# Adjacency turned by the DMA engines from a bf16 DRAM scratch, in place of TensorE turns through PSUM

## Chip, cores, metric

One NeuronCore of a Trainium2 chip runs the whole program. Times are device microseconds of that core; lower is better. Each kernel has four to nine runs, and its median is quoted. Ratios are the mean time of one kernel's fast runs over that of the other's of the same rounds, so not quite the ratio of the medians.

## The reference, cut to what matters

A stack of four graph attention layers over 16 graphs of 1024 nodes with 256 features. All layers of a graph use the same 1024 x 1024 adjacency, given as int32.

```python
# layers 0 to 2, each (activation and slope differ):
e = act(f1[:, :, None] + f2[:, None, :])          # (B, N, N)
e = where(adj == 0, -inf, e);  att = softmax(e, -1)
x = x + einsum('bij,bjo->bio', att, h)
# layer 3: the same with four heads, then a layer norm for each head
```

The kernel keeps attention weights with the neighbour j on the partitions, so it needs the mask turned: `mask[j, i]` from `adj[i, j]`. The adjacency of this input is symmetric, but the kernel may not count on it.

## The kernel before

The turn lies in `load`. A tile of 128 rows is loaded and cast to bf16 by the DMA, ScalarE sums (a - 0.5)^2 as a check that all entries are 0 or 1, TensorE turns eight 128 x 128 blocks into PSUM, and ScalarE copies them to the uint8 mask.

```python
def load(b):
    xs[b] = nodes.tile([P, NI, D], F32, name="x_b")
    nc.sync.dma_start(xs[b], x[b]...)
    masks[b] = nodes.tile([P, NI, N], U8, name="mask")      # three buffers
    def fetch(i):
        fetched[i] = adjs.tile([P, N], BF, name="adj_i")    # three buffers
        nc.gpsimd.dma_start(fetched[i], adj[b, ts(i, P), :])
    for i in range(AHEAD): fetch(i)                         # AHEAD = 2
    yield
    for i in range(NI):                                     # NI = 8
        if i + AHEAD < NI: fetch(i + AHEAD)
        adj_i = fetched.pop(i)
        every = wide.tile([P, N], BF, name="wide")
        nc.scalar.activation(every, adj_i, AF.Square, bias=minus_half,
                             accum_out=squares[:, b, i : i + 1])
        turned = psum.tile([P, NI, P], BF, name="misc", bufs=3)
        for j in range(NI):
            nc.tensor.transpose(turned[:, j, :], adj_i[:, ts(j, P)], ident_b)
        nc.scalar.copy(masks[b][:, :, ts(i, P)], turned)
        yield
```

`load(b + 2)` is advanced one step at each of the eight head steps of layer 3 of batch b. Two batches run interleaved. Instructions of an engine run in the order in which the program was built, and that order is not the program text's: work is placed where it was expected to be ready.

```python
# weigh: on VectorE, 8 of these for a half of 512 nodes
nc.vector.scalar_tensor_tensor(w[:, j, :], r, c(j), mask[:, j, ts(half, HALF)],
                               op0=op, op1=ALU.mult)                    # L255
# project: GpSimd makes 1/sqrt(var), ScalarE copies the turned activations (hT)
nc.gpsimd.tensor_tensor(r, r, minus_half.to_broadcast([P, n]), op=ALU.pow)   # L212
nc.scalar.copy(hT, turned)                                                   # L232
# layer 3, head step n
accT = ...8 matmuls...;  nc.scalar.copy(sums, accT);  next(coming, None);  yield 7.5
acc = ...4 turns of sums...;  inv = small.tile([P, NG], F32, name="inv4")
inverse(inv, acc[:, :, E])
```

Of the kernel before, what the change touches and what calls it, by code (L numbers as in the profile page):

```python
# [32 lines left out]
BF = mybir.dt.bfloat16  # L33
# [3 lines left out]
AF = mybir.ActivationFunctionType  # L37
# [3 lines left out]
P = 128  # L41
# [17 lines left out]
def short_path(ctx: ExitStack, tc: tile.TileContext, ins: dict, out: bass.AP, bad: bass.AP):  # L59

    nc = tc.nc
    x, adj = ins["x"], ins["adj"]
    B, N, D = x.shape
    H, T, E = ins["L3_a_src"].shape
    NI = N // P
# [5 lines left out]
    AHEAD = 2  # L71
    LAG = 120.0

    const = ctx.enter_context(tc.tile_pool(name="const", bufs=1))
    nodes = ctx.enter_context(tc.tile_pool(name="nodes", bufs=3))
    adjs = ctx.enter_context(tc.tile_pool(name="adjs", bufs=3))
    wide = ctx.enter_context(tc.tile_pool(name="wide", bufs=3))
    psum = ctx.enter_context(tc.tile_pool(name="psum", bufs=2, space=bass.MemoryType.PSUM))

    ident = const.tile([P, P], F32, name="ident")  # L80
    make_identity(nc, ident)
    ident_b = const.tile([P, P], BF, name="ident_b")
    nc.vector.tensor_copy(ident_b, ident)
    minus_half = const.tile([P, 1], F32, name="minus_half")
    nc.vector.memset(minus_half, -0.5)
    ones = const.tile([P, P], F32, name="ones")
# [2 lines left out]
    squares = const.tile([P, B, NI], F32, name="squares")  # L89
# [3 lines left out]
    xs, masks = {}, {}  # L93

    def load(b: int):

        xs[b] = nodes.tile([P, NI, D], F32, name="x_b")
        nc.sync.dma_start(xs[b], x[b].rearrange("(i p) f -> p i f", p=P))
        masks[b] = nodes.tile([P, NI, N], U8, name="mask")
        fetched = {}  # L100

        def fetch(i: int):

            fetched[i] = adjs.tile([P, N], BF, name="adj_i")
            nc.gpsimd.dma_start(fetched[i], adj[b, ts(i, P), :])  # L105

        for i in range(AHEAD):
            fetch(i)
        yield
        for i in range(NI):  # L110
            if i + AHEAD < NI:
                fetch(i + AHEAD)
            adj_i = fetched.pop(i)

            every = wide.tile([P, N], BF, name="wide")
            nc.scalar.activation(
                every, adj_i, AF.Square, bias=minus_half, accum_out=squares[:, b, i : i + 1]
            )
            turned = psum.tile([P, NI, P], BF, name="misc", bufs=3)
            for j in range(NI):  # L120
                nc.tensor.transpose(turned[:, j, :], adj_i[:, ts(j, P)], ident_b)
            nc.scalar.copy(masks[b][:, :, ts(i, P)], turned)
            yield


# [8 lines left out]
    bias = const.tile([P, D], F32, name="bias")  # L134
# [4 lines left out]
    for _ in load(0):  # L139
        pass  # L140
# [136 lines left out]
    def batch(b: int):  # L277
        xb, mask = xs.pop(b), masks.pop(b)
        coming = load(b + 2) if b + 2 < B else iter(())

        def begin(l: int):
# [164 lines left out]
    def stream(first: int):  # L446
        if first:
            for _ in load(first):
                yield 2.0
        for b in range(first, B, 2):  # L450
            yield from batch(b)
# [314 lines left out]
def tile_gat4(  # L766
# [27 lines left out]
    nc.vector.memset(ones, 1.0)  # L794
    n_bad = flags.tile([1, 1], I32, name="n_bad")
    short_path(tc, ins, out, bad)
    with tc.tile_pool(name="flag_psum", bufs=1, space=bass.MemoryType.PSUM) as psum:
        bads = psum.tile([1, 1], F32, name="bads")
# [39 lines left out]
```

## Time and profile before

| | before |
|---|---|
| median | 3343.4 us (3341.4 to 3344.3) |
| profiled span | 3341.3 us |
| first attention weights (L255) begin | 44.5 us |
| first output store issued | 360.3 us |
| from there to the end | 2981.0 us |

The prediction below shows the lines of the profile that it rests on.

### The profile page before, as it was taken

What the parts mean: (1) busy time and instruction counts of PE and PEld (TensorE: products, weight loads), DVE (VectorE), ACT (ScalarE), POOL (GpSimd) and SP (SyncE); (2) the same over time, 40 slices, a digit from 0 to 9 for tenths busy, and PEclk for the clock granted to TensorE, in tenths of its full rate; (3) what the DMA queues carried; (4) which work ended last, traced back from release to release, by engine and by line L of the source; (5) the groups of instructions that cost most, each with busy time, mean ns of one, the idle gap of its engine ahead of it and who ended that gap; (6) DMA issues with size and microseconds to landing.
All of it is one profiled execution on the core that took longest, in us unless ns stands there. A gap on an engine that the chain in (4) does not pass through costs nothing.

```text
span 3341.3 us, 38569 instructions
## 1 busy us (share of the span) xinstructions
PE 3103.0 (93%) x13702; PEld 2107.8 (63%) x13702; DVE 2504.0 (75%) x6140; ACT 974.3 (29%) x2081; POOL 1091.2 (33%) x1286
## 2 busy tenths in 40 slices
PE   6899999999989999899998999989999899998987
PEld 5765756657656675665756667566666666656652
DVE  5677787777778777787777877778777787777766
ACT  3423323232232322323233232332323223232121
POOL 1223324233242332424234142242323423234242
PEclk9999999999999999999999999999999999999998
DMA  4101101011010110101011010010101101000000
GB/s 115 26 4 16 32 11 40 7 17 29 13 39 8 16 29 13 38 10 16 26 16 35 10 42 4 13 35 13 39 4 17 32 13 38 7 10 13 1 13 14
DMA packets 55192, 73.19 MB, mean 22 GB/s; under 512 B 4049, under 2 KB 37969, under 8 KB 54993
## 3 DMA queue, kind: packets, MB, share of 16 engines
q0 software_dynamic: 18432, 33.56, 6.7%
q1 hardware_dynamic: 36560, 37.10, 3.5%
q8 instruction: 110, 1.80, 0.2%
q14 instruction: 90, 0.73, 0.1%
HBM read 87.43 MB, written 16.78 MB: 31 GB/s over the span
## 4 chain that ended last, share of the span: by engine, by line
DVE 45%; PE 42%; POOL 5%; ACT 4%; issue 3%; DMA 1%; SPq 0%; ACTq 0%; POOLq 0%; DVEq 0%
DVE weights L255 25%; PE acc L338 18%; PE acc L414 11%; PE projected L236 10%; DVE above L226 3%; PE misc L230 3%; DVE above L273 2%; DVE stats L220 2%; DVE above L274 2%; POOL x_b L275 2%; DVE V L290 2%; DVE y L380 1%; POOL y L379 1%; POOL rstd L212 1%; ACT below L271 1%
## 5 line engine op out<-in xcount | busy, mean ns | idle before, releaser
L338 PE MATMUL acc<-V,weights 128*128 128x257 f32 x6144 | 1454.9, 385 | 12.5 <-DVE weights L255 11.5
L338 PEld LDWEIGHTS acc<-V,weights 128*128 128x128 f32 x6144 | 1137.8, 191 | 208.9 <-DVE weights L255 47.2
L414 PE MATMUL acc<-weights,V 128*65 128x512 f32 x2048 | 914.2, 593 | 0.3 <-DVE weights L255 0.3
L255 DVE SCALAR_TENSOR_TENSOR weights<-row,ex,mask 128x512 f32<-128x512 f32 x1024 | 762.7, 784 | 2.7 <-ACT row L251 0.9
L255 DVE SCALAR_TENSOR_TENSOR weights<-row,V,mask 128x512 f32<-128x512 f32 x768 | 559.4, 776 | 53.0 <-ACT row L251 52.9
L414 PEld LDWEIGHTS acc<-weights,V 128*65 128x65 f32 x2048 | 278.7, 138 | 492.7 <-issue 474.0
L212 POOL TENSOR_TENSOR rstd<-rstd,minus_half 128x2 f32<-128x2 f32 (+1 forms) x320 | 311.3, 975 | 745.7 <-DVE rstd L211 703.2
L236 PE MATMUL projected<-W,hT 128*128 128x259 f32 (+1 forms) x2048 | 521.8, 398 | 14.8 <-ACT hT L232 11.3
L236 PEld LDWEIGHTS projected<-W,hT 128*128 128x128 f32 x2048 | 383.5, 195 | 130.1 <-ACT hT L232 60.4
L275 POOL TENSOR_TENSOR x_b<-x_b,above 128x256 f32<-128x256 f32 x256 | 227.5, 890 | 585.8 <-DVE above L274 532.5
L230 PE MATMUL misc<-ident,above 128*128 128x128 f32 x1024 | 189.1, 289 | 155.3 <-DVE above L226 108.6
L271 ACT ACTIVATE below<-acc,inv 128x256 f32<-128x256 f32 x256 | 120.0, 472 | 607.4 <-DVE inv L264 497.0
L232 ACT COPY hT<-misc 128x512 f32<-128x512 f32 x256 | 149.1, 586 | 495.8 <-PE misc L230 494.8
L230 PEld LDWEIGHTS misc<-ident,above 128*128 128x128 f32 x1024 | 113.7, 143 | 256.0 <-DVE above L226 120.3
L220 DVE BATCH_NORM_STATS2 stats<-x_b 128x6 f32<-128x256 f32 x512 | 206.7, 414 | 83.1 <-POOL x_b L275 78.9
L263 DVE TENSOR_SCALAR inv<-acc 128x1 f32<-128x1 f32 x256 | 37.3, 150 | 272.5 <-PE acc L338 272.3
L418 ACT COPY sums<-acc 65x512 f32<-65x512 f32 x128 | 74.0, 578 | 546.2 <-PE acc L414 546.1
L226 DVE TENSOR_SCALAR above<-x_b,mv 128x256 f32<-128x256 f32 x512 | 222.0, 443 | 3.8 <-POOL x_b L275 1.7
L105 POOL DMA_DIRECT2D adj_i<-in_adj_dram x128 | 77.1, 603 | 406.3 <-ACT sums L418 174.4
L290 DVE TENSOR_SCALAR V<-projected,rstd,V 128x256 f32<-128x256 f32 x256 | 134.8, 537 | 63.9 <-ACT V L286 62.9
L286 ACT ACTIVATE V<-projected,rstd 128x3 f32<-128x3 f32 x384 | 99.4, 261 | 262.0 <-PE projected L236 220.1
L314 POOL TENSOR_TENSOR x_b<-x_b,beta 128x256 f32<-128x256 f32 x128 | 117.3, 923 | 150.7 <-DVE above L226 148.6
(70 smaller groups left out, 2370.1 us busy)
## 6 DMA issues: line engine op xcount, KB each, us to landing
adj_i<-in_adj_dram POOLq DMA_DIRECT2D x128, 256.0 KB, 3.8
x_b<-in_x_dram SPq DMA_DIRECT2D x16, 1024.0 KB, 7.8
out_dram<-y SPq DMA_DIRECT2D x32, 512.0 KB, 3.8
W<-in_L_gnn_W_dram SPq DMA_DIRECT2D x3, 256.0 KB, 3.0
a_b<-in_L_gnn_a_dram SPq DMA_DIRECT2D x3, 256.0 KB, 6.4
a_b<-in_L_gnn_a_src_dram SPq DMA_DIRECT2D x1, 640.0 KB, 7.5
a_b<-in_L_gnn_a_dst_dram SPq DMA_DIRECT2D x1, 640.0 KB, 9.4
W<-in_L_gnn_W_dram SPq DMA_DIRECT2D x2, 128.0 KB, 8.9
```

What stands on the lines that cost most here:

```text
L212: nc.gpsimd.tensor_tensor(r, r, minus_half.to_broadcast([P, n]), op=ALU.pow)
L220: nc.vector.bn_stats(stats, xb[:, 2 * pair + n, :])
L226: nc.vector.tensor_scalar(above, xb[:, 2 * pair + n, :], mv[:, n, 0:1], 0.0, op0=ALU.subtract, op1=ALU.max)
L230: nc.tensor.transpose(turned[:, k, ts(n, P)], above[:, ts(k, P)], ident)
L232: nc.scalar.copy(hT, turned)
L236: nc.tensor.matmul(projected, hT[:, k, ts(n, P)], W[l][:, k, :], start=(k == 0), stop=(k == NK - 1),)
L255: nc.vector.scalar_tensor_tensor(w[:, j, :], r, c(j), mask[:, j, ts(half, HALF)], op0=op, op1=ALU.mult)
L271: nc.scalar.activation(below, acc[:, :D], AF.Exp, scale=inv)
L275: nc.gpsimd.tensor_add(xi, xi, above)
L290: nc.vector.tensor_scalar(V[:, i, :D], projected[:, :D], rstd, V[:, i, D : D + 1], op0=ALU.mult, op1=ALU.mult,)
L338: nc.tensor.matmul(acc, w[:, j, ts(i % NG, P)], V[:, j, : D + 1], start=(j == 0), stop=(j == NI - 1),)
L414: nc.tensor.matmul(accT, V3[:, j, h, :], w[:, j, :], start=(j == 0), stop=(j == NI - 1))
```

## The change

The intent is to free TensorE, the fullest engine, of 1024 turns, and ScalarE of reading PSUM, and to let the idle DMA engines turn. A cast to bf16 goes from DRAM to a DRAM scratch (four casts for a batch, issued by GpSimd). SyncE then issues eight turned loads of it. One such load of 128 columns by 1024 rows is called a strip here. A strip reads all rows, so it needs all four casts.

```diff
--- before.py
+++ after.py
@@ -76,11 +76,10 @@
     adjs = ctx.enter_context(tc.tile_pool(name="adjs", bufs=3))
     wide = ctx.enter_context(tc.tile_pool(name="wide", bufs=3))
     psum = ctx.enter_context(tc.tile_pool(name="psum", bufs=2, space=bass.MemoryType.PSUM))
+    dram = ctx.enter_context(tc.tile_pool(name="dram", bufs=2, space=bass.MemoryType.DRAM))
 
     ident = const.tile([P, P], F32, name="ident")
     make_identity(nc, ident)
-    ident_b = const.tile([P, P], BF, name="ident_b")
-    nc.vector.tensor_copy(ident_b, ident)
     minus_half = const.tile([P, 1], F32, name="minus_half")
     nc.vector.memset(minus_half, -0.5)
     ones = const.tile([P, P], F32, name="ones")
@@ -97,29 +96,29 @@
         xs[b] = nodes.tile([P, NI, D], F32, name="x_b")
         nc.sync.dma_start(xs[b], x[b].rearrange("(i p) f -> p i f", p=P))
         masks[b] = nodes.tile([P, NI, N], U8, name="mask")
+
+        narrow = dram.tile([N, N], BF, name="narrow")
+        for q in range(4):
+            nc.gpsimd.dma_start(narrow[ts(q, 2 * P), :], adj[b, ts(q, 2 * P), :])
         fetched = {}
 
-        def fetch(i: int):
-
-            fetched[i] = adjs.tile([P, N], BF, name="adj_i")
-            nc.gpsimd.dma_start(fetched[i], adj[b, ts(i, P), :])
-
-        for i in range(AHEAD):
-            fetch(i)
+        def fetch(j: int):
+            fetched[j] = adjs.tile([P, N], BF, name="adj_j")
+            nc.sync.dma_start_transpose(fetched[j], narrow[:, ts(j, P)])
+
         yield
-        for i in range(NI):
-            if i + AHEAD < NI:
-                fetch(i + AHEAD)
-            adj_i = fetched.pop(i)
+        for j in range(AHEAD):
+            fetch(j)
+        for j in range(NI):
+            if j + AHEAD < NI:
+                fetch(j + AHEAD)
+            adj_j = fetched.pop(j)
 
             every = wide.tile([P, N], BF, name="wide")
             nc.scalar.activation(
-                every, adj_i, AF.Square, bias=minus_half, accum_out=squares[:, b, i : i + 1]
-            )
-            turned = psum.tile([P, NI, P], BF, name="misc", bufs=3)
-            for j in range(NI):
-                nc.tensor.transpose(turned[:, j, :], adj_i[:, ts(j, P)], ident_b)
-            nc.scalar.copy(masks[b][:, :, ts(i, P)], turned)
+                every, adj_j, AF.Square, bias=minus_half, accum_out=squares[:, b, j : j + 1]
+            )
+            nc.scalar.copy(masks[b][:, j, :], adj_j)
             yield
 
 
```

## The prediction

> **What bounds the kernel now.** I read the page's engine totals first, then the totals by window, the groups by line, the waits of TensorE, and the timeline around one group of turns.
>
> ```profile
> PE 3103.0 (93%) x13702; PEld 2107.8 (63%) x13702; DVE 2504.0 (75%) x6140; ACT 974.3 (29%) x2081; POOL 1091.2 (33%) x1286
> ...
> DVE 45%; PE 42%; POOL 5%; ACT 4%; issue 3%; DMA 1%; SPq 0%; ACTq 0%; POOLq 0%; DVEq 0%
> ```
>
> TensorE is busy 93% of the span, yet the chain that ended last passes as often over VectorE (45%) as over TensorE (42%). So TensorE is the fullest engine, but time taken off it is not all time taken off the end: part turns into waits for VectorE. ScalarE (29%) and GpSimd (33%) have room.
>
> ```profile
> 0.00:45.00 45.00, 18.59 (x113) 15.58 (x114) 18.11 (x87) 25.31 (x41) 9.93 (x21) 1.00 0.82 213
> 45.00:3341.00 3296.00, 3084.44 (x13591) 2092.18 (x13589) 2485.86 (x6054) 949.00 (x2040) 1081.30 (x1265) 0.99 0.09 19
> ```
>
> The windows (columns: TensorE, its weight loads, VectorE, ScalarE, GpSimd, clock, DMA share, GB/s) show two regimes. In the first 45 us the DMA engines are 82% busy and TensorE has little to do: the start is a load. After that TensorE is 3084.44/3296 = 93.6% busy, with some 212 us idle, and the DMA engines are 9% busy. There is a great deal of DMA room for a turn that moves there.
>
> ```profile
> L121 PE MATMUL misc<-ident_b,adj_i 128*128 128x128 bf16 x1024 | 86.2, 226 | 27.2 <-DVE ident_b L83 13.8 <-DMA adj_i<-in_adj_dram 12.9 <-ACT row L251 0.5
> L116 ACT ACTIVATE wide<-adj_i,minus_half 128x1024 bf16<-128x1024 bf16 x128 | 145.7, 1138 | 7.4 <-DMA adj_i<-in_adj_dram 7.4
> L122 ACT CAST mask<-misc 128x1024 uint8<-128x1024 bf16 x128 | 128.8, 1008 | 63.4 <-PE misc L121 63.4
> ```
>
> The turns that go away are L121: 1024 of them, 226 ns in the record. That duration is not what one costs, because matmuls overlap. The timeline of TensorE around one group shows the real price:
>
> ```profile
> 639.69 1.88 PE L414 MATMUL acc<-weights,V 128*65 128x512 f32 x4
> 641.41 0.61 PE L121 MATMUL misc<-ident_b,adj_i 128*128 128x128 bf16 x8
> 641.86 1.95 PE L338 MATMUL acc<-V,weights 128*128 128x257 f32 x8
> ```
>
> The eight turns start at 641.41 and the next matmul starts at 641.86: 0.45 us for eight, 56 ns for one. Other whole groups repeat this 0.447 us.
>
> ```profile
> PE misc L230 <- DVE above L226: 108.6, 129, 3.1
> PE misc L230 <- DVE mv L221: 29.0, 13, 2.8
> ...
> PE misc L230 <- ACT mask L122: 1.9, 1, 1.9
> PE misc L423 <- ACT mask L122: 1.8, 7, 0.3
> ```
>
> TensorE's waits after 50 us (total us, times, longest) are nearly all for the layer norm on VectorE ahead of the turns of L230. Waiting for the PSUM buffer that the mask copy of L122 holds is a few us in all.
>
> **What the Trainium skill says.** (1) "VectorE: DVE Perf Modes", section "The three transpose paths": a 128x128 bf16 turn is given 390 ns on TensorE and 1309 ns by the DMA crossbar. The trace has 226 ns for one on TensorE and a pitch of only 56 ns inside a stream, so the table's 390 ns overstates what this change removes about sevenfold. (2) "DMA: Bandwidth & Descriptors", section "Latency and other measured facts", gives the DMA transpose 261 GB/s where the middle dimension isn't contiguous. The two disagree: by (2) a 1024x128 turn (262 KB) is 1.0 us of data, by (1) taken eight times it is 10.5 us. No transpose is in the trace of before, so nothing decides. (3) Same page, section "Anatomy of one DMA — SWDGE (gpsimd) path": about 2.0 us fixed plus bytes over 436 GB/s. For one tile of adjacency (512 KB read) that is 3.2 us; the trace says 3.8 us to landing, near enough. (4) Same page, section "Two DMAs through the same engine are not ordered": the transpose may be issued only after the cast's completion is seen, so their latencies add. Every turned column strip reads all 1024 rows, so it waits for all four casts of its batch.
>
> **The change part by part.**
>
> Removed from TensorE: 1024 turns x 56 ns = 57 us in all, of which 960 lie after the start (the profile counts 960 after 40 us): 960 x 56 ns = 54 us. Not all comes off the end: with 212 us idle already there and VectorE on 45% of the chain, I choose 60 to 65% as realised, between 48% (TensorE's part of TensorE plus VectorE on the chain, 42 of 87) and the 93.6% that its occupancy suggests. That is -34 us.
>
> Removed waits: no adjacency turn occupies a "misc" PSUM buffer any more. The waits for L122 seen on TensorE and its loads are 1.9 + 1.8 + 1.8 and 3.5 + 3.5 + 2.2 us, the pairs overlapping, so about 6 us. -5 us.
>
> ScalarE: the mask copy reads SBUF bf16 in place of PSUM. L116 does the same size from SBUF in 1138 ns against 1008 ns for L122, so at most 128 x 0.13 = +17 us on an engine idle 71% of the time. 0 us on the path. The squares are summed over columns in place of rows, at the same cost.
>
> GpSimd: 128 issues of 603 ns become 64 of twice the rows. At the worst twice the time each, so 77 us stays 77 us, off the path. Its waits ahead of L105 (406.3 us in the page) fall away, but where I looked the next GpSimd instruction was released by VectorE after that, so they cost nothing. 0 us.
>
> DMA: the casts took 6.7% of sixteen engines' span, 224 us, 14 us a batch. They now write DRAM. To these come 128 turned strips, 1.0 us each by (2), 10.5 us by (1); I take 2.5 us as an estimate between the two, weighted to the first: 8 x 2.5 = 20 us a batch. Together about 34 us of DMA time in a batch's 3341/16 = 209 us. Even at 10.5 us it would be 98 us, and fit. The throughput is hidden.
>
> Latency in the steady state: ScalarE runs in order, and the squares and mask copies of a batch wait for casts (14 us or more) and then the strips. In the trace of before, the first squares of a batch ran at 563.73 and their mask copy at 642.09, so such work is placed tens of us ahead of need. If the order built for the new kernel places a square slightly before its strip lands, ScalarE stands still, and behind it are row copies and hT copies that TensorE and VectorE need. I put 2 us of stall on each of 16 batches, of which a third counts: 16 x 0.7 = +11 us.
>
> Start: before, the adjacency tiles came one after another, the last mask copy of batch 0 began at 34.17 us, and the first weights (L255) at 44.52, eight of them spread to about 50. Now the four casts share busy DMA engines with W, x and the constants: landing at 22 to 25 us. Then eight strips at 2.5 us, +3 us of first latency and 2 us for ScalarE: 24 + 20 + 3 + 2 = 49 us for the last mask. It is needed at about 50, so nearly all of the 15 us fits in slack, while the x and a loads that share the engines come later. I put +8 us.
>
> Sum: 3343.65 - 34 - 5 + 0 + 11 + 8 = 3323.65. Call it **3323 us**, 0.6% faster.
>
> **Rivals.** A: the gain is realised in full and nothing is given back (ScalarE's slack hides everything). For it: TensorE 93.6% busy after the start, DMA 9%. Against it: the VectorE half of the chain. It makes 3343.65 - 57 - 6 = 3281 us, still within 2%. To be over 2% faster it would need more than TensorE spends on these turns, by a better order of everything else.
>
> B: the DMA turn is as slow as the table's 1309 ns a block. Then eight strips are 84 us, the start is longer by 24 + 84 + 5 - 50 = about 63 us, and each batch stalls ScalarE by much more: at 10 us counted a batch +160 us. With -39 us gained that is around 3343 + 63 + 160 - 39 = 3527 us, slower by 5%. For it: the skill's table. Against it: the bandwidth figure of the other page, and that the work lies far ahead of its use.
>
> C: VectorE's chain alone sets the end, and TensorE's 54 us all turn into waiting on L226 and L255. Then only the start counts: 3343 + 8 + 11 - 5 = 3357 us. For it: VectorE first on the chain with weights L255 alone 25%. Against it: TensorE idle only 6.4% after the start, and its waits for L255 only 11.5 us.
>
> **Range and chances.** Rival A bounds the fast side at 3281; a lucky order may give 15 us more: low 3266. The slow side holds C and a mild form of B, where the start costs 30 us and stalls 50 us: 3343 + 80 - 39 = 3384, rounded up: high 3395. Faster by over 2% (under 3276.8) 0.09; slower by over 2% (over 3410.5), which is B, 0.14; within 2% 0.77.
>
> **What would show each step.** TensorE's busy time after should fall to about 3103 - 86 = 3017 us, with L121 gone and the span falling by less. The waits of L230 for L226 should grow by some 20 us over 108.6; if they grow by 50, C was right. ScalarE's waits for the DMA of adj_j after the start should be under 40 us; hundreds would be B. The landing of one strip should be 3 to 6 us from issue; over 10 is B. The first weights (L255) should begin by 55 us. The prediction is wrong if the strips land much later than that, if SyncE holds strips behind output stores, or if the new order of instructions moves other waits by more than 60 us.

## The result, and the profile after

The changed kernel takes 3472.3 us (3462.1 to 3477.5, four runs), a ratio of 1.0383 (95% interval 1.0357 to 1.0408): 3.8% slower, outside the range that the prediction gave. The page of the changed kernel, its busy times, its chain, its DMA queues and its DMA issues:

```profile
PE 3051.4 (88%) x12678; PEld 2059.0 (59%) x12678; DVE 2496.7 (72%) x6139; ACT 980.9 (28%) x2081; POOL 1042.0 (30%) x1222
...
q1 hardware_dynamic: 171728, 70.67, 8.8%
q0 software_dynamic: 2048, 33.56, 4.5%
...
DVE 40%; PE 37%; ACT 7%; POOL 5%; DMA 4%; another core or an unknown queue 4%; issue 2%; SPq 1%; ACTq 0%; POOLq 0%; DVEq 0%
...
narrow<-in_adj_dram POOLq DMA_DIRECT2D x64, 512.0 KB, 19.4
...
adj_j<-narrow SPq DMA_TRANSPOSE x128, 3.5
```

The turns left TensorE as planned, and a strip lands 3.5 us after its issue, well inside the 3 to 6 us that the prediction allowed. So the DMA turn is not slow. But the chain now has 4% of DMA against 1% before, and 7% of ScalarE against 4%. Where they lie shows in the totals by window, cut where the first weights begin (columns as in the prediction: TensorE, weight loads, VectorE, ScalarE, GpSimd, clock, DMA share, GB/s):

```profile
0.00:204.30 204.30, 14.92 (x48) 11.82 (x49) 17.37 (x85) 25.81 (x42) 35.03 (x74) 1.00 0.97 212
204.30:3468.30 3264.00, 3036.53 (x12632) 2047.14 (x12630) 2479.29 (x6055) 955.10 (x2041) 1007.00 (x1148) 0.98 0.08 19
```

The first weights come at 204.3 us, not 44.5. In all that time the DMA engines are 97% busy and TensorE works 15 us. After it 3264.0 us remain, against 3341.3 - 44.5 = 3296.8 before. So the change gains 32.8 us after the first weights and loses 159.8 us ahead of them: 159.8 - 32.8 = 127.0 us, which is the difference of the spans. Cut at the first output store it is the same picture. The stores in SyncE's timeline, of the kernel before and of the changed one:

```profile
360.26 1.92 SPq L439 DMA_DIRECT2D out_dram<-y  x2
```

```profile
511.58 0.94 SPq L438 DMA_DIRECT2D out_dram<-y  x2
```

That is +151.3 us for the start, and 3468.3 - 511.6 = 2956.7 us from there against 2981.0: -24.3 us.

What fills the start? The casts' own line in the changed kernel, and what GpSimd waited for ahead of them:

```profile
L102 POOL DMA_DIRECT2D narrow<-in_adj_dram x64: 486/486/719, 1.4 to 166.7; - x64
...
  DMA narrow<-in_adj_dram: 95.5, 48
```

All 64 casts, of all 16 batches, are issued between 1.4 and 166.7 us. The only thing that a cast waits for is that an earlier cast lands. The change asks for a pool of two scratch buffers, but no cast waits for a strip: the ninth cast, the first beyond two batches, is issued at 9.79 us, and the first strip is read only from 45.05 us on. As the results are correct, each batch must have had a scratch of its own; the trace leaves buffer numbers out, so this is inferred. Most strips of batch 0 meet this flood. The first four slipped through in a pause of it: GpSimd stood 34.07 us before an `rstd` of the layer norm and issued no cast between 22.4 and 57.7 us. The timelines of ScalarE and of TensorE there:

```profile
61.54 1.03 ACT L121 CAST mask<-adj_j 128x1024 uint8<-128x1024 bf16 x1
146.37 1.15 ACT L118 ACTIVATE wide<-adj_j,minus_half 128x1024 bf16<-128x1024 bf16 x1 [83.80 <-DMA adj_j<-narrow]
147.43 0.19 ACT L118 ACTIVATION_READ_ACCUMULATOR wide<-adj_j,minus_half 128x1 f32 x1
147.52 1.03 ACT L121 CAST mask<-adj_j 128x1024 uint8<-128x1024 bf16 x1
148.45 1.55 ACT L231 COPY hT<-misc 128x512 f32<-128x512 f32 x3
```

```profile
149.08 3.82 PE L235 MATMUL projected<-W,hT 128*128 128x259 f32 x8 [84.01 <-ACT hT L231]
```

ScalarE stands 83.80 us before one strip. The hT copies behind it in its order had been ready since about 65 us, and TensorE waits 84.01 us for them. One strip took 84 us here against 3.5 us later. The trace's DMA packets say why. Between 62 and 146 us (counted from the packets in the trace file, not a view of the profile):

```
queue              packets of data   bytes each   median duration
casts (q0)         547               32768        2431 ns
strips (q1)        1024              256          18 to 31 ns
```

A strip is 1024 packets of 256 B, 64 for each of the sixteen engines. The casts are runs of 32 KB (33.56 MB in 1024 packets; the other 1024 of the page's 2048 have 4 bytes) that hold an engine 2.43 us. In those 84 us an engine passed 34 cast packets and 64 strip packets, about two small ones to each large one. 34 x 2.43 = 83 us. Away from the flood (600 to 3000 us) the 1024 packets of a strip pass in 1.4 us.

After the start, two waits grew. TensorE's longest (it all lies after 204.3 us), and ScalarE's for strips after 204.3 us:

```profile
PE misc L229 <- DVE above L225: 159.2, 157, 2.8
```

```profile
ACT mask L121 <- DMA adj_j<-narrow: 89.9, 57, 4.4
```

TensorE's wait was 108.6 us before. Before, ScalarE waited only 2.5 us for DMAs after its first 45 us.

### The profile page after: what moved, and what is told of

Same layout as the page of the kernel before. It is cut to its first block, busy times and chain, and to the rows that moved or that the text cites. A ratio compares the mean times of both kernels' runs of the same rounds, so it can differ in the third digit from the quotient of the medians.

```text
span 3468.3 us, 36630 instructions
## 1 busy us (share of the span) xinstructions
PE 3051.4 (88%) x12678; PEld 2059.0 (59%) x12678; DVE 2496.7 (72%) x6139; ACT 980.9 (28%) x2081; POOL 1042.0 (30%) x1222
## 3 DMA queue, kind: packets, MB, share of 16 engines
q0 software_dynamic: 2048, 33.56, 4.5%
## 4 chain that ended last, share of the span: by engine, by line
DVE 40%; PE 37%; ACT 7%; POOL 5%; DMA 4%; another core or an unknown queue 4%; issue 2%; SPq 1%; ACTq 0%; POOLq 0%; DVEq 0%
DVE weights L254 23%; PE acc L337 16%; PE acc L413 10%; PE projected L235 8%; DMA adj_j<-narrow 4%; DVE above L225 3%; PE misc L229 2%; DVE above L272 2%; DVE stats L219 2%; POOL x_b L274 2%; DVE above L273 1%; ACT wide L118 1%; DVE V L289 1%; ACT mask L121 1%
## 5 line engine op out<-in xcount | busy, mean ns | idle before, releaser
L254 DVE SCALAR_TENSOR_TENSOR weights<-row,V,mask 128x512 f32<-128x512 f32 x768 | 561.7, 778 | 48.1 <-ACT row L250 46.6
L229 PE MATMUL misc<-ident,above 128*128 128x128 f32 x1024 | 196.8, 296 | 163.4 <-DVE above L225 159.2
L118 ACT ACTIVATE wide<-adj_j,minus_half 128x1024 bf16<-128x1024 bf16 x128 | 145.6, 1138 | 122.9 <-DMA adj_j<-narrow 122.9
L378 POOL TENSOR_TENSOR y<-y,bias 128x512 f32<-128x512 f32 x64 | 89.6, 1400 | 298.5 <-DVE y L425 278.8
L272 DVE TENSOR_SCALAR above<-acc,inv 128x256 f32<-128x256 f32 x256 | 121.6, 478 | 65.2 <-ACT below L270 64.2
```

The source lines that it names most:

```text
L118: nc.scalar.activation(every, adj_j, AF.Square, bias=minus_half, accum_out=squares[:, b, j : j + 1])
L229: nc.tensor.transpose(turned[:, k, ts(n, P)], above[:, ts(k, P)], ident)
L272: nc.vector.tensor_scalar(above, acc[:, :D], inv, 0.0, op0=ALU.mult, op1=ALU.max)
```

## The experiments

**Theory 1, the start:** nothing holds the casts back, the flood of 64 makes the start 150 us longer, and the rest gains. Rivals: the loss is spread over the run; the sum of bytes; the strips' own latency. **Theory 2, the rest:** TensorE's 57 us come off nearly in full, but ScalarE, working in order, stands before strips that have not landed and gives part back. Rival: VectorE's chain gives it back.

| kernel | median us | ratio to before | first weights | first output | from there to the end |
|---|---|---|---|---|---|
| before | 3343.4 | 1 | 44.5 | 360.3 | 2981.0 |
| changed | 3472.3 | 1.0383 | 204.3 | 511.6 | 2956.7 |
| e1_two_scratch | 3356.6 | 1.0037 | 81.2 | 398.8 | 2960.8 |
| e8_one_scratch | 3349.7 | 1.0018 | 69.7 | 391.1 | 2961.5 |
| e2_row_packets | 3472.7 | 1.0385 | 174.6 | 515.4 | 2956.0 |
| e7_hybrid_flood | 3399.6 | 1.0164 | 69.6 | 440.3 | 2957.9 |
| e3_hybrid | 3322.7 | 0.9940 | 46.6 | 360.5 | 2960.8 |
| e10_late_strips | 3299.7 | 0.9871 | 45.8 | 360.1 | 2937.9 |
| e9_plain_strips | 3309.4 | 0.9896 | 45.9 | 360.9 | 2950.3 |
| e5_turns_twice | 3396.9 | 1.0167 | 48.0 | 369.6 | 3023.2 |
| e4_no_turn | 3404.9 | 1.0182 | 43.1 | 359.5 | 3043.0 |
| e11_no_turn_late | 3309.6 | 0.9901 | 44.1 | 352.2 | 2955.2 |
| e12_before_late | 3344.7 | 1.0007 | 46.5 | 363.3 | 2980.5 |

The last three columns are from each kernel's one profiled run. All results were correct.

### e1_two_scratch: a scratch that is used again

```diff
+    scratch = [dram.tile([N, N], BF, name=f"narrow_{k}", bufs=1) for k in range(2)]
...
-        narrow = dram.tile([N, N], BF, name="narrow")
+        narrow = scratch[b % 2]
```

> The changed kernel, but with two DRAM scratches made once and used in turn, so that a batch's casts must wait until the strips of two batches earlier have been read. Theory (the loss is all in the start, because nothing held the 64 casts of all 16 batches back and the first strips had to share the DMA engines with them): the first weights come at 60 to 80 us in place of 204 us, the stretch from there to the end stays near 3264 us, the time is 3325 to 3350 us. Rival (the loss is spread over the run, by strips landing late or waits that took the place of the turns): the time stays over 3420 us.

3356.6 us: 116 us of the loss are gone by this alone. The rest of the run (2960.8 us from the first output) is within 4 us of the changed kernel's, so the loss lay in the start and in the casts' order. By the expectation's own measure, from the first weights, the rest is 3278.4 us, 14 us more than 3264: that much lies between first weights and first output. The expected 3325 to 3350 us was missed by 7 us: eight casts still come ahead of the first strips, and the first weights at 81.2 us are just past the range.

### e8_one_scratch: four casts ahead in place of eight

Against e1 the edit comes to this:

```diff
-        narrow = scratch[b % 2]
+        narrow = scratch[0]
```

> As e1_two_scratch, but with one scratch, so that only the 4 casts of batch 0 come ahead of its strips (8 in e1, 64 in the changed kernel). Theory (the start grows with the casts that run ahead of the first strips, some 2.5 us each): first weights at 62 to 75 us against 81 us in e1 and 204 us, and 3338 to 3352 us. Rival (the rest of the start's loss is the strips' own latency): first weights at 78 us or later, time as e1 or worse.

First weights at 69.7 us, time 3349.7 us, both in the range of the theory. Four casts fewer brought the first weights 11.5 us earlier, 2.9 us a cast. With 4, 8 and 64 casts that nothing holds back the start is 69.7, 81.2 and 204.3 us: the 56 more of the changed kernel cost 123 us, 2.2 us each.

### e2_row_packets: the same flood in small packets

```diff
-        narrow = dram.tile([N, N], BF, name="narrow")
+        narrow = dram.tile([N, N + P], BF, name="narrow")
...
-            nc.gpsimd.dma_start(narrow[ts(q, 2 * P), :], adj[b, ts(q, 2 * P), :])
+            nc.gpsimd.dma_start(narrow[ts(q, 2 * P), :N], adj[b, ts(q, 2 * P), :])
```

> The changed kernel with all its casts still issued at the start, but rows of the scratch padded by 128 elements, so that a cast can't be cut into runs of 32 KB and goes row by row. Theory of the packets (a strip's packet of 256 B waits behind a cast's packet of 32 KB that holds the engine 2.4 us, some 34 of them for one strip): a strip beside the casts takes 10 us or less in place of 84 us, the first weights come at 90 to 130 us, the time is 3350 to 3400 us. Rival theory (the sum of the bytes counts, and the strips are through only when the casts are): first weights still at 170 us or later, time 3435 to 3475 us.

The cast packets were now 2 KB of 172 ns, and the strip in the flood went from 84 to 11.2 us, close to what the packet theory said (two, which landed at 91 and 116 us, still took some 24 us). ScalarE's timeline, one strip after the other:

```profile
126.82 1.15 ACT L118 ACTIVATE wide<-adj_j,minus_half 128x1024 bf16<-128x1024 bf16 x1 [9.04 <-DMA adj_j<-narrow]
...
138.01 1.15 ACT L118 ACTIVATE wide<-adj_j,minus_half 128x1024 bf16<-128x1024 bf16 x1 [9.01 <-DMA adj_j<-narrow]
...
149.20 1.15 ACT L118 ACTIVATE wide<-adj_j,minus_half 128x1024 bf16<-128x1024 bf16 x1 [9.02 <-DMA adj_j<-narrow]
```

11.2 us is 64 strip packets of an engine, each behind one cast packet: 64 x 0.172 = 11.0. Yet the time did not move (3472.7 us), so my expectation of 3350 to 3400 us was wrong and the rival's range held. The first weights came at 174.6 us, 30 us earlier than in the changed kernel, but the first output 4 us later. A likely reason, which no run separates: ScalarE's order has the 16 strips of batches 0 and 1 among the first batch's work, and 16 x 11.2 = 179 us is about as long as the flood (last cast issued at 188 us). By this reading the cut of the packets decides which strip is late, not when the first two batches are through. The cure that e1 and e8 show is fewer casts ahead; smaller packets cured nothing.

### e3_hybrid and e3_again: TensorE turns the first two batches

`load` is that of the kernel before for batches 0 and 1, and that of e1 for the others. The first casts into each scratch are held back:

```diff
+    def load(b: int):
+        return load_by_pe(b) if b < 2 else load_by_dma(b)
...
         V = yield from attend(0, V, finish0, 1)
+        if b < 2:
+            gate = small.tile([P, 2], BF, name="gate", bufs=2)
+            nc.gpsimd.tensor_copy(gate, xb[:, NI - 1, :2])
+            for q in range(4):     # a few bytes in each quarter, ahead of its cast
+                nc.sync.dma_start(scratch[b][q * 2 * P : q * 2 * P + 16, :2], gate[:16, :])
```

> Batches 0 and 1 are turned by TensorE as in the kernel before (it idles in the start anyway), batches 2 to 15 by the DMA engines through two scratches used in turn, and the casts of batches 2 and 3 are held back by a write of a few bytes into the scratch that comes after layer 0 of batches 0 and 1. Theory: the start is that of before (first weights at 43 to 50 us) and 14 batches gain 2.0 to 2.2 us each, so 3308 to 3322 us, faster than both. Rival (the gain after the start in the changed kernel was only that casts were out of the way, all done early; beside casts in the steady state it is lost): 3338 us or more.

> The hybrid a second time, beside e10 on the same chip: 3318 to 3328 us, and what e10 gains over it is read from the same rounds.

3322.7 us, and 3321.8 us when run again: the start is that of before (first weights at 46.6 us, first output at 360.5), and 0.6% is gained. The time after the first output, 2960.8 us, is within 4 us of the changed kernel's, so casts running beside the work cost next to nothing there; that rival falls. 14 batches gained 21 us, 1.5 us each, a quarter less than the 2.0 to 2.2 that I wrote, and the time lies just past the end of my range.

### e7_hybrid_flood: the flood without strips that wait

As e3_hybrid, without the gate and with `narrow = dram.tile(...)` for each batch again.

> As e3_hybrid (batches 0 and 1 turned by TensorE), but every batch has a scratch of its own and nothing holds the casts back, so that all 56 run in the first part of the run while no strip is needed. It takes the strips away from the flood of casts. Theory (the flood itself harms whatever is loaded in the start, also adjacency tiles and constants that share the DMA engines and the queue): first weights at 80 to 130 us, 3360 to 3420 us. Rival (only strips are harmed, by their small packets): first weights within 10 us of e3_hybrid's 46.6 us, 3310 to 3335 us.

3399.6 us, 77 us slower than e3_hybrid. The time is in the theory's range, but neither view of the mechanism was right. First weights at 69.6 us are earlier than the theory said, yet the first output is 80 us late. Most of that lies after the first weights, and the waits show another road. GpSimd, ScalarE and TensorE in its timeline:

```profile
118.12 0.49 POOL L135 DMA_DIRECT2D narrow<-in_adj_dram  x1 [2.04 <-DMA narrow<-in_adj_dram]
118.62 0.73 POOL L247 TENSOR_TENSOR rstd<-rstd,minus_half 128x2 f32<-128x2 f32 x1
119.38 0.42 ACT L321 ACTIVATE V<-projected,rstd 128x3 f32<-128x3 f32 x2 [31.01 <-POOL rstd L247]
...
122.65 0.69 PE L265 MATMUL misc<-ident,above 128*128 128x128 f32 x2 [28.08 <-DVE above L261]
```

GpSimd issues a cast, waits some 2 us for an earlier one to land, and issues the next. The small `rstd` of the layer norm stands behind a row of them in its order. ScalarE waited 31.01 us for it, and TensorE then 28.08 us. So a flood also harms by blocking the engine that issues it.

### e5_turns_twice: more turns on TensorE

```diff
                 nc.tensor.transpose(turned[:, j, :], adj_i[:, ts(j, P)], ident_b)
+                nc.tensor.transpose(turned[:, j, :], adj_i[:, ts(j, P)], ident_b)
```

> The kernel before with each adjacency turn done twice into the same place: 57 us of TensorE work added (1024 x 56 ns), nothing else. It measures how much of a change in TensorE's turns reaches the end. Theory (about 60%, as the prediction chose): 3371 to 3384 us. Rival (VectorE sets the end): under 3355 us. TensorE alone sets it: 3395 us or more.

3396.9 us against 3344.1 us: +53 us for 57 us added, 93%. It lies past the 60% range, just inside "TensorE alone". So time added to TensorE reaches the end almost in full, and that VectorE is first on the chain of before did not mean that it hides such time. That time taken away comes off in full does not follow; e10 and e11 measure that.

### e4_no_turn and e11_no_turn_late: no turn anywhere

Right only because this input is symmetric.

```diff
-            turned = psum.tile([P, NI, P], BF, name="misc", bufs=3)
-            for j in range(NI):
-                nc.tensor.transpose(turned[:, j, :], adj_i[:, ts(j, P)], ident_b)
-            nc.scalar.copy(masks[b][:, :, ts(i, P)], turned)
+            nc.scalar.copy(masks[b][:, i, :], adj_i)
```

> The kernel before with no turn at all: the mask is copied straight from the adjacency as loaded (right here only because this input's adjacency is symmetric). It takes TensorE's 57 us away and adds no DMA work. Theory (some 60% of TensorE's time comes off the end): 3300 to 3315 us. Rival C of the prediction (VectorE sets the end, TensorE's time turns into waits): 3335 to 3345 us. Full realisation: under 3290 us.

3404.9 us, 1.8% slower though all the turns are gone. All three expectations missed. The waits between 400 and 3000 us point to the cause; e4_no_turn's for ScalarE:

```profile
ACT mask L117 <- DMA adj_i<-in_adj_dram: 197.2, 96, 3.8
```

Without the turn between load and mask copy, ScalarE's copy stands right where the load was expected to have landed, and it had not, 96 times in that stretch. e11 takes that wait away and leaves the rest. For batches from 2 on, the two ScalarE instructions read their bias from a tile made out of the last head step's sums:

```diff
+                late = small.tile([P, 2], F32, name="late", bufs=2)
+                nc.gpsimd.tensor_scalar(late[:, 0:1], after[0], 0.0, -0.5, op0=ALU.mult, op1=ALU.add)
+                nc.gpsimd.tensor_scalar(late[:, 1:2], after[0], 0.0, None, op0=ALU.mult)
+                half, zero = late[:, 0:1], late[:, 1:2]
...
+                nc.scalar.activation(masks[b][:, i, :], adj_i, AF.Identity, bias=zero)
...
             inverse(inv, acc[:, :, E])
+            after[0] = inv[:, 0:1]
```

> As e4_no_turn (no turn at all), with ScalarE's two instructions on a tile tied to the head step before as in e10. Theory (e4 was slow because ScalarE stood before tiles that had not landed, 219 us, and GpSimd before tiles that ScalarE had not freed, 284 us, with work for TensorE queued behind both): ScalarE's wait for tiles goes to under 20 us and the time to 3290 to 3315 us. Rival (without the turns something else slows the run): still over 3370 us.

3309.6 us, 95 us faster than e4_no_turn. ScalarE no longer waits for a tile between 400 and 3000 us; it waits 42 us for `late`. GpSimd's waits for tiles that ScalarE had not freed stayed, in the same stretch, of e4 and then of e11:

```profile
POOL adj_i L103 <- ACT wide L114: 223.7, 36, 7.8
```

```profile
POOL adj_i L104 <- ACT wide L121: 228.7, 37, 7.8
```

So it was ScalarE's wait for the DMA that cost e4 its time, and not GpSimd's. But with no turn anywhere e11 is only 33 us faster than before (3342.6 us in the same rounds), 58% of the 57 us, and 10 us slower than e10 below, which turns every batch.

### e9_plain_strips: what turning costs over a plain load

Against e3_hybrid:

```diff
-            nc.sync.dma_start_transpose(fetched[j], narrow[:, ts(j, P)])
+            nc.sync.dma_start(fetched[j], narrow[ts(j, P), :])
```

> As e3_hybrid, but each strip is a plain load of 128 rows of the scratch in place of a turned load (right only because this input's adjacency is symmetric). It tells what the turning costs over a plain load of the same bytes. Theory (the turn is hidden; only ScalarE's waits for the strip count a little): within 10 us of e3_hybrid's 3322 us. Rival (turned strips disturb the steady state): under 3308 us.

3309.4 us, 13 us faster than e3_hybrid (not in the same rounds, but each against its own runs of before: ratios 0.9896 and 0.9940): between the two ranges. The issues, of e3_hybrid and of e9, say that the turned strip lands 0.7 us later:

```profile
adj_i<-narrow SPq DMA_TRANSPOSE x112, 3.4
```

```profile
adj_i<-narrow SPq DMA_DIRECT2D x112, 256.0 KB, 2.7
```

ScalarE's wait for strips between 400 and 3000 us goes with it, from 86.6 us to 53.6 us. What shows of the turning is this later landing, where ScalarE already waits. The casts also land sooner beside plain strips, 5.9 us after their issue against 8.4; what that is worth was not separated.

### e10_late_strips and e12_before_late: strips read one step later

e10 is e3_hybrid with the same `late` tile in `load_by_dma`: `bias=late[:, 0:1]` for the squares, `AF.Identity, bias=late[:, 1:2]` for the mask copy.

> As e3_hybrid, but the two ScalarE instructions on a strip read their bias (-0.5 and 0) from a small tile that GpSimd makes out of the sums of the head step before, so that they stand in ScalarE's order one step later, when the strip has long landed. Cost: two tiny GpSimd instructions a strip. Theory (after the start, the rest of TensorE's 57 us is given back because ScalarE, which works in order, stands before strips that have not landed, 87 us in e3): that wait goes to under 10 us and the time to 3295 to 3312 us. Rival (VectorE's chain gives it back): 3316 to 3330 us, while the wait is gone all the same.

3299.7 us (3298.5 to 3300.3), ratio 0.9871 (0.9856 to 0.9886): 1.3% faster than before, and 22 us faster than the hybrid in the same rounds. The waits of the mask copy between 400 and 3000 us, of e3_again and of e10:

```profile
ACT mask L156 <- DMA adj_i<-narrow: 83.2, 58, 4.6
```

```profile
ACT mask L160 <- POOL late L155: 28.0, 34, 1.9
```

The wait for strips is gone altogether; shorter ones for `late`, 28.0 us here and 18.4 us ahead of the squares, took part of its place. The theory's range was hit. The control is the kernel before with the same tie:

> Control for e10: the kernel before, with its TensorE turns, with the same small bias tiles that tie ScalarE's two instructions to the head step before (batches 2 to 15). Theory (e10's gain over e3 is the removed wait for strips, and the kernel before has no such wait after its start): within 8 us of before, 3335 to 3352 us. Rival (the tie itself makes a better order of the whole, whatever turns the adjacency): under 3330 us.

3344.7 us, ratio 1.0007 (0.9990 to 1.0024): no gain. The tie does not make a better order by itself; it helps where ScalarE stands before a DMA.

## Why the prediction was wrong

The step that failed is the **start**: "Now the four casts share busy DMA engines with W, x and the constants ... I put +8 us." It took the casts as one batch's, as many as the program text has in one `load`. All 64 were issued in the first 167 us. Measured: +160 us to the first weights, +151 us to the first output. e1, which only makes the scratch be used again, gives 116 us back. e3 gives the whole start back.

- **The price of the turns**, 56 ns each and 57 us in all, held: e5 adds as many and pays 53 us.
- **"60 to 65% as realised"**: its reason, that the rest turns into waits for VectorE, is not shown. Time added comes out at 93% (e5). In e10, 14 batches have 14 x 64 x 56 ns = 50 us less on TensorE, and 43 us came off: 85%. The hybrid gave back 29 of the 50 us, and 22 of them returned when ScalarE's wait for strips was taken away. But e11, where all 57 us are gone, realises 58%, and why it falls behind e10 is open.
- **The granted clock**, which neither the prediction nor the experiments looked at, may be part of this. The traces record it in stretches, at 1.0 or 0.5. Between 400 and 3000 us it stood at 0.5 for 37.5 us before, 37.5 in e5 and 41.0 in e12, but for 61.4 us in the changed kernel, 75.1 in e3_again, 88.7 in e10, 105.8 in e11 and 139.9 in e4. So the kernels that lost turns have more of it. TensorE's busy time for the same 12678 matmuls grows too, from 3051.4 us (changed, mean clock 0.985) to 3068.3 (e11, 0.978) and 3090.2 (e4, 0.973). No run separates this from the waits.
- **ScalarE's stalls**: I expected under 40 us of waiting after the start and +11 us of cost. It waited 89.9 us; in the hybrid, taking the wait away brought 22 us over 14 batches. So this term was half of what it is.
- **Steady state in sum**: -34 - 5 + 11 = -28 us predicted; measured -24.3 us after the first output, -32.8 us after the first weights. The sum is right by luck: the gain and the stalls were each put too small, and the two errors cancel.
- **A strip's landing**: 3.5 us, inside the 3 to 6 us. The 2.5 us of DMA time that I took for each was too much: its packets pass in 1.4 us, nearer the 1.0 us of the prediction's lower figure. The 10.5 us of rival B is not seen.
- **GpSimd "0 us"** holds in the steady state. In a flood it does not: e7's `rstd` stood 31 us behind casts.
- **TensorE's busy time** fell by 51.6 us, not 86: the records of the 86.2 us overlap those of their neighbours, as the timeline in the prediction shows. The pitch (57 us in all) was the figure to use.
- Rival B named about 5% slower, but by slow turns and stalls spread over the batches. The result was near it in size and not in cause. Rival C, in which none of TensorE's time comes off, is ruled out by e10 and e11, which gain 43 and 33 us by taking turns away. TensorE's wait for L226 grew by 51 us, which the prediction called the sign of C; that sign was badly chosen, because in e10 it is still 120.8 us between 400 and 3000 us (80.3 before) while the gain is there.

Still open: how the start's 151 us divide between late constants (the loads ahead of the first strip kept SyncE until 45 us; before they were through by 13 us), the strips in the flood, and GpSimd's order. e2 changed the second, and with it the first (SyncE came to its first strip at 31.6 us), and the first output did not come earlier; so they may cover one another. A fourth buffer for strips, which might let them land earlier, was not run.

## What to carry to other kernels

When a transfer is taken from a place where a buffer held it back, ask what holds it back now: if nothing does, all of them may be issued at the start, ahead of the few that the start needs. An engine that works in order must not stand in front of a DMA that has only just been issued: tie its instruction to something later that is ready anyway. And price a turn on TensorE by its pitch in the stream, not by its record: here 56 ns, not 226.

## What the Trainium skill lacked or had wrong

- "VectorE: DVE Perf Modes", section "The three transpose paths", gives 390 ns for a 128 x 128 bf16 turn on TensorE and 1309 ns by the DMA crossbar. In a stream a turn cost TensorE 56 ns, and e5 pays 53 us for 1024 more. A turned strip of eight such blocks landed 3.4 to 3.5 us after its issue, 0.7 us later than a plain load of as many bytes (2.7 us), and its packets pass in 1.4 us. So the table can't be multiplied by the number of blocks: eight times 1309 ns would be 10.5 us.
- "DMA: Bandwidth & Descriptors", section "Queues, rings and completion order", says that an engine goes round its queues packet by packet. In the runs the packets of the two queues do alternate, about two of a strip to one of a cast in the changed kernel and one to one in e2. But the page doesn't say what it costs when packets differ in size: strip packets of 256 B beside casts of 32 KB (2431 ns) made a strip take 84 us in place of 3.5; beside 2 KB (172 ns) 11.2 us.
- No page that I read says that a cast from DRAM to DRAM with whole contiguous rows goes in packets of 32 KB (1024 of them for the 33.56 MB of the changed kernel), and that padding the scratch's rows brings packets of 2 KB (e2).
- No page that I read says that a row of DMAs issued by GpSimd blocks its small arithmetic: in e7 `rstd` came 31 us late, because each cast is issued only when an earlier one has landed.
